# Two layers of graph attention on one core: the order in which layer 1's masks are loaded

## The chip, the core and the metric

One core of a Trainium2 chip runs the whole kernel in one launch. Its engines are TensorE (PE, with PEld for its weight loads), VectorE (DVE), ScalarE (ACT), GpSimd (POOL) and SyncE (SP), which here does nothing but issue DMAs; 16 DMA engines move the data. Each engine runs its own instructions in order and waits on semaphores for the others. The metric is the device time of one execution, in microseconds.

## The reference

`x` is 16 batches of 1024 nodes with 512 features, `adj` a 1024 x 1024 matrix with about one sixteenth of its entries set, all float32.

```python
# layer 0
h = relu(layernorm(x))
x = x + (adj @ h) @ weight + bias
# layer 1, with adj as the mask
u = relu(layernorm(x))
h = u @ W
e = leaky_relu((h @ a1)[:, :, None] + (h @ a2)[:, None, :], 0.2) * adj
att = softmax(e, axis=2)
x = x + elu(att @ h + beta * h)
```

The product of scores and mask is a plain multiplication, so each batch's 1024 x 1024 softmax needs the whole of `adj` (4 MB) again.

## The kernel before

The kernel handles layer 0 batch after batch, then layer 1 batch after batch. The change lies in layer 1. For each batch `b` there are two phases on TensorE. `layer1_a` multiplies the attention matrix by `u` (results named `z`), `layer1_b` multiplies the result by `W` (results named `pq`). Both use a scheme of seven products of half-size blocks instead of eight, in the order p1, p5, p2, p6, p7, p3, p4 for the weights and p1, p2, p6, p5, p7, p3, p4 for the attention. Each product has two parts, so a phase has 14 steps, numbered 0 to 13. The sums that the scheme needs of the right operand are T1 to T4 (tiles `pT_T`); T4 is built late, its first half after step 9 and its second after step 10 of `layer1_a` (`LATE_A`, line 1166), and product p4 reads it in steps 12 and 13.

While TensorE works on batch `b`, the other engines prepare the softmax of batch `b + 1`. Its work is cut into named pieces, which tables place behind numbered steps: `SOFTMAX_A` (line 1159) in `layer1_a`, `SOFTMAX_B` and `LOGITS_B` (lines 1164 and 1165) in `layer1_b`. A table's place fixes the order of the pieces on every engine. The pieces are:

- `L`: load the logits' two vectors. `L0` to `L7`: load one mask, 128 rows of 1024 numbers (512 KB), into the pool `ld`, which has two buffers of 4 KB per partition. `e0` to `e7`: the same load into the pool `b4`, which has 12 buffers of 4 KB, shared with the scores and the sums of `z` (lines 1150 and 1151).
- `M0` to `M7` (`masked`, line 753): ScalarE writes the scores `e` in four pieces, VectorE multiplies them by the mask and keeps the row maximum `mx`.
- `X` and `x` (`spread_max`): after M3 and after M7, the maxima of four blocks go to DRAM (`md`) and come back spread (`mall`), five DMAs. `N` and `n` (`top`) take the final maximum on VectorE (`nm`).
- `E0` to `E7`: exponentials on ScalarE, with row sums. `V0` to `V7`: transposes on VectorE into `pT`. `S` and `s` spread the sums (`sd`, `sall`), as `X` does.

SP gets all DMAs of these pieces in one order. With them stand, in `layer1_a`, the stores of the batch before (`out_dram<-o`, four DMAs after each of steps 3 to 6, line 923) and the loads of `u` (`ul_U`); in `layer1_b` of batches 1 to 8 a late row of batch 15 (`late`), which is loaded, normalised and stored again. POOL issues four DMAs per batch that add `x1d` to the output (`o<-x1d`, line 916), which run from the end of `layer1_b` into `layer1_a`. SP also waits, before most DMAs, for the DMA eight places earlier, since eight semaphores serve them in turn.

A load names its buffer's pool like this:

```python
def load(self, g, pl=None, tag="ld"):
    self.mask[g] = (pl or ld).tile([P, N], F32, tag=tag, name=f"mask_{self.b}_{g}")
    sp.dma_start(out=self.mask[g], in_=maskd[g])
```

The pool gives a new tile the buffer that came free, and the load waits until the last reader of that buffer is done. Nearly every instruction is recorded through one helper, so the profile shows line 118 throughout, and the tiles' names tell the instructions apart.

Of the kernel before, what the change touches and what calls it, by code (L numbers as in the profile page):

```python
# [65 lines left out]
def kernel(  # L66
# [12 lines left out]
    B, N, D = x.shape  # L79
# [996 lines left out]
    def merged(*plans):  # L1076
        out = {}
        for plan in plans:
            for k, steps in plan.items():
                out.setdefault(k, []).extend(steps)  # L1080
        return out
# [57 lines left out]
    def plan_softmax(order, s):  # L1139
        names = {  # L1140
            "L": [s.logits], "B": [s.blocks, 0], "b": [s.blocks, 1],
            "X": [s.spread_max, 0], "x": [s.spread_max, 1], "N": [s.top, 0], "n": [s.top, 1],
            "S": [s.spread_sum, 0], "s": [s.spread_sum, 1],
            "D": [s.diagonal, 0], "d": [s.diagonal, 1],
        }
        for g in range(NCH):
            names[f"M{g}"] = [s.masked, g]
            names[f"E{g}"] = [s.exp, g]
            names[f"V{g}"] = [s.turn, g]
            names[f"L{g}"] = [s.load, g]  # L1150
            names[f"e{g}"] = [s.load, g, b4, "b4"]
            names[f"K{g}"] = [s.keep, g]
            names[f"R{g}"] = [s.reload, g]
        for n in ("T1", "T2", "T3", "T4"):
            for k in range(2):
                names[n + "ab"[k]] = [s.right_sum, n, k]
        return {k: [tuple(names[n]) for n in steps.split()] for k, steps in order.items()}

    SOFTMAX_A = {
        0: "M0 L2 M1 L3", 1: "M2 L4", 2: "M3 L5 X", 3: "M4 L6", 4: "M5 L7", 5: "N B E0",  # L1160
        6: "M6 E1 V0", 7: "M7 x V1", 8: "E2", 9: "E3 V2 S", 10: "n b V3 E4", 11: "E5 V4",
        12: "E6 V5", 13: "E7 V6 V7 s",
    }
    SOFTMAX_B = {0: "D", 1: "T1a", 2: "T1b", 4: "d", 5: "T2a", 6: "T2b"}
    LOGITS_B = {8: "L", 11: "L0", 12: "L1"}
    LATE_A = {5: "T3a", 6: "T3b", 9: "T4a", 10: "T4b"}


# [21 lines left out]
    for b in range(B):  # L1190
# [14 lines left out]
        else:  # L1205
# [4 lines left out]
            plans_b += [  # L1210
                plan_softmax(FIRST_B, sms[0]), plan_softmax(LOGITS_B, sms[1]),
            ]
# [24 lines left out]
    for b in range(B):  # L1237
# [16 lines left out]
        if b + 2 < B:  # L1254
            plan_b = merged(plan_b, plan_softmax(LOGITS_B, sms[b + 2]))
        if 1 <= b <= NCH:
# [46 lines left out]
```

## Time and profile before

| | us |
|---|---|
| median of 3 runs | 2292.17 (2292.01 to 2292.51) |
| profiled execution | 2291.31 |
| its span, first to last instruction | 2289.5 |
| first `z` matmul of batch 0 | 1098.42 |
| last matmul | 2279.95 |

Times in the views count from the start of the span. Layer 1 is thus the second half, 16 batches. The granted TensorE clock was 0.998 of full speed. In the views, a line has the start, the duration, the engine, the operation, and the tiles as written and read; in square brackets stands how long the engine stood idle before it and what ended that wait. "SPq" lines are DMA issues, whose duration is that of issuing, not of the transfer. In the list of waits, a line gives the waiting engine and tile, what it waited for, the total in us, how often, and the longest. Idle time of an engine other than the bound costs nothing by itself.

### The profile page before, as it was taken

Reading aid. Unit: us, or ns where it says so; the run is one execution under the profiler, and the core shown is the slowest. Engines: PE = TensorE matmul, PEld = TensorE weight load, DVE = VectorE, ACT = ScalarE, POOL = GpSimd, SP = SyncE. Lnnn points to the kernel's source line nnn. Section 1 sums busy time; section 2 is a strip of 40 time slices with the busy share of each in tenths; the row PEclk is TensorE's granted clock in tenths of the full one; section 3 lists DMA queues with packets and bytes.
Section 4 is the critical chain, followed back from the end, with each engine's and each line's share of the span. In section 5 each row is a group of like instructions: output and inputs, shape, how many; then the busy total and the mean of one; then the engine's idle time right before and its main releaser. Section 6 shows DMA issues by size and latency. Waiting matters only on the chain.

```text
span 2289.5 us, 29757 instructions
## 1 busy us (share of the span) xinstructions
PE 2253.4 (98%) x8524; PEld 1609.9 (70%) x8524; DVE 1842.7 (80%) x4285; ACT 1540.5 (67%) x4106; POOL 244.0 (11%) x508
## 2 busy tenths in 40 slices
PE   9999999999999999999999999999999999999998
PEld 5888888888888888888566546664566556664565
DVE  7888888988888888889877777787678776787664
ACT  3776776777777767666577577766767677766653
POOL 1211111121111111110000000000000000000000
PEclk9999999999999999999999999999999999999999
DMA  7343454343344434336555566546655655446541
GB/s 215 130 139 120 139 169 157 129 148 127 123 148 157 163 133 149 98 109 210 168 138 143 152 172 165 145 144 170 177 142 144 178 154 147 133 133 167 160 122 54
DMA packets 194292, 336.03 MB, mean 147 GB/s; under 512 B 78800, under 2 KB 86992, under 8 KB 194128
## 3 DMA queue, kind: packets, MB, share of 16 engines
q1 hardware_dynamic: 185168, 302.15, 40.9%
q0 software_dynamic: 8640, 31.46, 7.4%
q8 instruction: 67, 1.10, 0.2%
q14 instruction: 97, 0.79, 0.1%
q10 hardware_dynamic: 320, 0.52, 0.1%
HBM read 228.33 MB, written 109.91 MB: 148 GB/s over the span
## 4 chain that ended last, share of the span: by engine, by line
PE 70%; DMA 12%; DVE 8%; ACT 5%; SPq 3%; issue 2%; POOL 1%; DVEq 0%; ACTq 0%; POOLq 0%
PE po_Y L118 9%; PE pq_Y L118 8%; PE y_Y L118 8%; PE z_Y L118 8%; DMA mask<-maskd 7%; PE po_X L118 5%; PE y_X L118 5%; PE pq_X L118 4%; DVE e L118 3%; DMA md<-mx 3%; SPq L118 3%; PE y_W L118 2%; PE pq_W L118 2%; PE y_p7y L118 2%; PE y_p3y L118 2%; PE po_W L118 2%
## 5 line engine op out<-in xcount | busy, mean ns | idle before, releaser
L118 ACT ACTIVATE e<-e,nm 128x256 f32<-128x256 f32 x480 | 237.1, 497 | 168.1 <-DVE nm L118 168.1
L118 DVE CUSTOM_DVE_ANT_0 e<-e,mask 128x256 f32<-128x256 f32 x512 | 190.8, 421 | 189.2 <-DMA mask<-maskd 161.8
L118 PE MATMUL z_Y<-pT,ul_U 128*128 128x512 f32 x512 | 224.9, 592 | 0.0
L118 ACT ACTIVATE e<-s2b,s1b 128x256 f32<-128x256 f32 x512 | 216.4, 500 | 0.0
L118 PE MATMUL po_Y<-w_c,y_C 128*128 128x256 f32 x768 | 188.3, 379 | 0.0
L118 PEld LDWEIGHTS z_Y<-pT,ul_U 128*128 128x128 f32 x512 | 97.1, 190 | 115.8 <-issue 112.0
L118 PE MATMUL pq_Y<-w_c,z_C 128*128 128x256 f32 x768 | 173.4, 379 | 0.0
L118 DVE CUSTOM_DVE_ANT_0 y_S<-xr,v_bc 128x512 f32<-128x512 f32 x240 | 165.2, 688 | 9.2 <-DVE s L118 0.5
L118 PEld LDWEIGHTS pq_Y<-w_c,z_C 128*128 128x128 f32 x768 | 145.9, 190 | 26.7 <-issue 7.7
L118 PEld LDWEIGHTS po_Y<-w_c,y_C 128*128 128x128 f32 x768 | 145.9, 190 | 20.3 <-ACT po_X L118 0.2
L118 DVE STREAM_TRANSPOSE pT<-e 128x512 f32<-128x512 f32 x240 | 155.5, 686 | 1.0
L118 PE MATMUL z_Y<-pT_T,ul_U 128*128 128x512 f32 x256 | 117.8, 605 | 20.1 <-DVE pT_T L118 20.1
L118 ACT ACTIVATE h<-h,nb_h,r_h 128x512 f32<-128x512 f32 (+1 forms) x132 | 98.2, 792 | 57.5 <-POOL nb_h L118 57.5
L118 POOL DMA_DIRECT2D o<-x1d x60 | 52.7, 936 | 620.7 <-DVE o L118 558.0
L118 ACT ACTIVATE y_S<-xr 128x512 f32<-128x512 f32 x90 | 56.7, 630 | 91.8 <-DVE xr L118 91.4
L118 PE MATMUL po_X<-w_c,y_S 128*128 128x256 f32 x512 | 115.7, 379 | 0.0
L118 PE MATMUL pq_X<-w_c,z_S 128*128 128x256 f32 x512 | 115.6, 379 | 0.0
L118 PE MATMUL z_X<-pT_T,ul_S 128*128 128x512 f32 x256 | 112.5, 592 | 0.0
L118 PE MATMUL z_W<-pT,ul_U 128*128 128x512 f32 x256 | 112.5, 592 | 0.0
L118 PE MATMUL z_Y<-pT_T,ul_S 128*128 128x512 f32 x256 | 112.5, 592 | 0.0
L118 PE MATMUL z_X<-pT,ul_S 128*128 128x512 f32 x256 | 112.5, 592 | 0.0
L118 PEld LDWEIGHTS z_Y<-pT_T,ul_U 128*128 128x128 f32 x256 | 48.0, 192 | 87.3 <-issue 52.7
(241 smaller groups left out, 5115.0 us busy)
## 6 DMA issues: line engine op xcount, KB each, us to landing
mask<-maskd SPq DMA_DIRECT2D x128, 512.0 KB
h<-in_x_dram SPq DMA_DIRECT2D x64, 512.0 KB
xr<-in_x_dram SPq DMA_DIRECT2D x256, 128.0 KB
x1d<-xr SPq DMA_DIRECT2D x64, 512.0 KB
ul_U<-ud_U SPq DMA_DIRECT2D x64, 512.0 KB
ud_U<-xr SPq DMA_DIRECT2D x60, 512.0 KB
o<-x1d POOLq DMA_DIRECT2D x60, 512.0 KB, 7.6
out_dram<-o SPq DMA_DIRECT2D x240, 128.0 KB
```

The source lines that it names most:

```text
L118: return lambda *args, **kwargs: tc.keep_in_program_order(f(*args, **kwargs))
```

## The change

Only two tables differ. The loads of masks 2 and 3 move into the weight product of the batch before, into `b4`; there `L0` and `L1` move two steps forward. Masks 4 and 5, still in `ld`, take the places of 2 and 3 behind M0 and M1. Masks 6 and 7 go into `b4` behind steps 1 and 2, ahead of the row maximum `X` and of the output's stores, which begin behind step 3. The tables are also used once at the end of layer 0, for batch 1's masks.

```diff
     SOFTMAX_A = {
-        0: "M0 L2 M1 L3", 1: "M2 L4", 2: "M3 L5 X", 3: "M4 L6", 4: "M5 L7", 5: "N B E0",
+        0: "M0 L4 M1 L5", 1: "M2 e6", 2: "M3 e7 X", 3: "M4", 4: "M5", 5: "N B E0",
         6: "M6 E1 V0", 7: "M7 x V1", 8: "E2", 9: "E3 V2 S", 10: "n b V3 E4", 11: "E5 V4",
         12: "E6 V5", 13: "E7 V6 V7 s",
     }
     SOFTMAX_B = {0: "D", 1: "T1a", 2: "T1b", 4: "d", 5: "T2a", 6: "T2b"}
-    LOGITS_B = {8: "L", 11: "L0", 12: "L1"}
+    LOGITS_B = {8: "L", 9: "L0", 10: "L1", 11: "e2", 12: "e3"}
     LATE_A = {5: "T3a", 6: "T3b", 9: "T4a", 10: "T4b"}
```

## The prediction

> **What bounds the kernel now.** I read the page's busy times first, then the waits, then the timelines of TensorE, VectorE and the DMA queue over one batch of layer 1, and last the busy table by stretches for the DMA engines.
>
> ```profile
> PE 2253.4 (98%) x8524; PEld 1609.9 (70%) x8524; DVE 1842.7 (80%) x4285; ACT 1540.5 (67%) x4106; POOL 244.0 (11%) x508
> ```
>
> ```profile
> DVE e L118 <- DMA mask<-maskd: 161.8, 50, 6.1
> ...
> PE z_Y L118 <- DVE pT_T L118: 20.1, 14, 3.0
> ```
>
> TensorE is the bound, so only its own gaps are worth anything: the 161.8 us that VectorE stands before missing masks count only where they make TensorE late. The last line says where: the matmuls of the right sum T4 (tile `pT_T`), 14 times. The page's 20.1 us is the gap alone; the loss is better taken from the distance between the first `z` matmuls of successive batches. Batches 0 and 1 take 72.24 us each (seven products of 6.87 and seven of 3.45 us) and have no gap. Batches 2 to 14 take 78.25, 74.38, 73.90, 73.28, 75.25, 75.02, 73.86, 73.41, 73.10, 73.47, 73.23, 74.28, 73.21: together 25.5 us over 72.24 each. That is all this change can take away; batch 15 prepares no softmax.
>
> I follow batch 3, whose first `z` matmul starts at 1321.15 ("rel 0"). TensorE first:
>
> ```profile
> 1362.35 1.88 PE L118 MATMUL z_Y<-pT_T,ul_U 128*128 128x512 f32 x4
> 1366.10 5.42 PE L118 MATMUL z_Y<-pT_T,ul_U 128*128 128x512 f32 x12 [1.87 <-DVE pT_T L118]
> ```
>
> Product p4 starts at rel 41.2 and uses the first half of T4 for 4 matmuls; the second half is due at 41.2 + 1.7 = rel 42.9, and comes at 44.9. VectorE shows why:
>
> ```profile
> 1335.55 0.42 DVE L118 CUSTOM_DVE_ANT_0 e<-e,mask 128x256 f32<-128x256 f32 x1 [5.04 <-DMA mask<-maskd]
> ...
> 1347.37 0.26 DVE L118 TENSOR_REDUCE nm<-mall 128x16 f32<-128x64 f32 x1 [0.51 <-DMA mall<-md]
> ...
> 1353.38 0.42 DVE L118 CUSTOM_DVE_ANT_0 e<-e,mask 128x256 f32<-128x256 f32 x1 [4.41 <-DMA mask<-maskd]
> ...
> 1359.87 1.20 DVE L118 TENSOR_TENSOR pT_T<-pT,pT_T 128x1024 f32<-128x1024 f32 x1
> ...
> 1364.83 1.22 DVE L118 TENSOR_TENSOR pT_T<-pT,pT_T 128x1024 f32<-128x1024 f32 x1
> ```
>
> M6 (1353.38) waits 4.41 us for its mask; behind it without a further wait stand V0, M7, V1, the reads of p7, T4's first half, V2, the reads of p3 and T4's second half. The queue shows why the mask is late:
>
> ```profile
> 1309.45 0.90 SPq L118 DMA_DIRECT2D mask<-maskd  x2
> ...
> 1328.35 11.85 SPq L118 DMA_DIRECT2D mask<-maskd  x4
> 1340.24 0.42 SPq L118 DMA_DIRECT2D md<-mx  x1
> 1344.32 1.74 SPq L118 DMA_DIRECT2D mall<-md  x4
> 1346.16 1.78 SPq L118 DMA_DIRECT2D out_dram<-o  x4
> 1348.05 0.38 SPq L118 DMA_DIRECT2D mask<-maskd  x1
> ```
>
> Masks 0 and 1 go early; 2 to 5 each wait for M0 to M3 to free one of the two `ld` buffers; 6 goes behind `mall` and an output store, though its buffer was free since M4. The DMA engines are idle just before and full in that stretch (the last two columns are DMA share and GB/s):
>
> ```profile
> 1314.00:1319.00 5.00, 5.00 (x25) 4.38 (x25) 4.27 (x8) 3.98 (x10) 1.82 (x4) 1.00 0.00 0
> 1325.00:1340.00 15.00, 15.00 (x36) 6.65 (x35) 7.53 (x36) 12.42 (x31) 2.60 (x3) 1.00 1.03 241
> ```
>
> **What the Trainium skill says.** "DMA: Bandwidth & Descriptors", section Queues, rings and completion order: a DMA engine consumes one ring's descriptors in ring order and takes turns between rows packet by packet. The trace agrees: mask packets and POOL's accumulating ones alternate from 1332 to 1334 (0.17 and 0.33 us each), and `md`, 8 KB, takes 4.1 us from issue to `mall` behind mask 5, where `sd`, equally small, took 1.4 us at 1299.76 on a quiet queue. "PSUM — Partial Sum Buffer", section Engine vs sequencer instructions, calls VectorE's queue strict FIFO; T4 behind M6 is that. "Perfetto Trace Analysis", section Optimization Strategy: the same gap repeating on the engine that should be saturated can mean too few buffers for the next tile; 13 batches with one gap at one place agree.
>
> **The change part by part.** No instruction and no byte is added. In the program's order, VectorE's, TensorE's and POOL's instructions stand as before; only SP's order, the 4 KB slots, and so some waits of SP and ScalarE, differ.
>
> (a) Masks 2 and 3 move up behind masks 0 and 1, at about 1310.4 and 1310.9, from 1328.35 and 1329.94. They pass the late row's store and then M0 and M1. Two masks took from 1310.5 to 1313.5, so these run to about 1316.5, in the idle stretch, and are there 10 us before M2. Their slots were last held by score tiles whose transposes end at about 1301: no wait. The late store (1319.11) finds the queue empty again. M2 and M3 then wait only for ScalarE, which writes their scores from 1329.85 and 1332.13: M3 ends at about 1332.13 + 0.45 + 1.6 = 1334.2 (rel 13.1) instead of rel 18.6.
>
> (b) Masks 4 and 5 take the places of 2 and 3 behind M0 and M1 (rel 7.2 and 8.8), so as those did they land at rel 14.4 and 17.2. ScalarE writes M4's and M5's scores at rel 14.4 and 17.9: cost nothing.
>
> (c) Masks 6 and 7 follow at once, at about rel 9.2 and 9.7, in slots whose TensorE readers ended in the weight product: no wait. They leave the stores' stretch (share 0.9 and more from 1350 to 1360). M6 waits only for ScalarE.
>
> (d) The row maximum `md`, issued at rel 13.2 instead of 19.1, now stands behind four masks. This is the unknown cost. From 1331.5 the engines have to move the rest of POOL's third accumulation and the fourth (2.6 us each, 128 packets of 0.33 us on 16 engines) and four masks (1.3 us each): 10.4 us, to about rel 20.8; with some 1 us for `md` itself it lands near rel 21.8. Before, its landing is `mall`'s issue, rel 23.2. At the low end `md` comes at rel 19, at the high end one mask later than before, 24.5; I take 1.3 us earlier than before. `mall` and the maxima follow at their old distance, so the first exponential, at rel 26.7 before, starts at 25.4.
>
> (e) From there ScalarE sets the pace. In batch 0, where masks weren't late, M6 starts 3.0 us after the first exponential (E0), M7 7.0 and T4 ends 17.1 us after it (E0 25.2, T4 42.3). So E0 by rel 42.9 - 17.1 = 25.8 leaves no gap. The old starts of E0 in batches 2 to 14 are 27.9, 26.7, 26.2, 25.8, 27.6, 27.6, 25.9, 25.8, 25.4, 26.2, 24.8, 26.3, 25.6. With (d)'s 1.3 us off, only batches 2, 6 and 7 are left over, by 0.8 + 0.5 + 0.5 = 1.8 us. With nothing off, 2.1 + 0.9 + 0.4 + 1.8 + 1.8 + 0.1 + 0.4 + 0.5 = 8.0 us remain.
>
> (f) New waits on ScalarE: M7's scores now go into mask 6's slot and wait for M6. In ScalarE's order E1 (2.0 us) and a copy (0.5) lie between M6's scores and M7's, M6's last piece on VectorE ends 0.4 us after its scores: hidden with 2 us to spare. If mask 6 were late, ScalarE would stop there, with E2, E3 and the copies of `z` behind it. The copy of p6 waits for the late store, landed some 12 us before: nothing.
>
> (g) Batch 0: masks 2 and 3 also pass the four `x1d` stores and the load of W1, due much later. The queue is full from rel -1.4 to 14.1 in both orders; masks 4 to 7 end near 19.3, `md` near 20.4 (before, `mall` at 21.3): no gap appears.
>
> Sum: 25.5 - 1.8 = 23.7, less 0.7 for spread between batches: 23.0 us. The profiled execution, 2291.31 us (span 2289.5), becomes 2268.3; the median of the runs is 0.86 above it, so 2269.2.
>
> **Rivals.** B, `md` gains nothing behind four masks: 8.0 us of gaps stay, 17.5 gained, 2274.7. For it: `md` in ring order; against: masks 2 and 3 run in an idle stretch. C, the gap refills: VectorE, freed, meets another late operand, or mask slots bind, and half or more stays: 2281 to 2292. Against it: slots resolve a step or more before their users, and batch 1, already without a gap, has T4 at 42.5. That the change doesn't bring masks earlier belongs here. D, slower: `md` much later behind four masks and the accumulations. The old T4 ends are on average 42.9 + 25.5/13 = rel 44.9, which E0 reaches at 27.8; old E0 is 26.3 on average, so it decides where `md` lands over 1.5 us later than before, at about rel 24 on average. At 2.5 us later, 13 batches lose 1.0 us each: 2305. For it: 2 MB now stand before `md`; against: nothing was added to those stretches and 1 MB left them.
>
> **How the numbers follow.** Likeliest, 0.62: 2266.7 (all 25.5 gone) to 2272, at 2269.2. B 0.20, 2272 to 2280. C 0.11, of which 0.05 still gains over 0.2% and 0.06 doesn't. D 0.07. 0.2%, 4.6 us, is about what a measurement of this kernel can tell from no change. Faster 0.62 + 0.20 + 0.05 = 0.87, same 0.06, slower 0.07. Range: 2266 to 2280 holds the first two.
>
> **What would show it.** Right: masks 2 and 3 issued with 0 and 1; no wait of M2, M3 and M6 for a mask; `mall` about 1.3 us earlier; batches of 72.2 to 73 us. Wrong: `mall` at rel 23 or later (B, D), or gaps of TensorE at another tile (C).

## The result and the profile after

| | before, us | after, us |
|---|---|---|
| median (range), 4 runs each | 2292.09 (2288.11 to 2292.51) | 2266.95 (2266.72 to 2267.59) |
| profiled execution | 2291.31 | 2266.74 |
| its span | 2289.5 | 2264.4 |
| batches 0 to 14, time beyond 72.24 us each, summed | 25.5 | under 0.1 |
| E0, mean of batches 2 to 14, rel | 26.30 | 24.51 |
| T4 ends, mean of the same, rel | 44.59 | 42.11 |

The changed kernel takes 0.9895 [0.9877, 0.9912] of the time before. The medians differ by 25.1 us, where 22.9 were forecast; all that layer 1 lost is gone. ("rel" is, as in the prediction, the time after a batch's first `z` matmul; E0 is the first exponential; T4's second half is due at rel 42.75, as a run below shows.)

The busy times of the page of the changed kernel, for the row shown of before:

```profile
PE 2248.3 (99%) x8524; PEld 1611.9 (71%) x8524; DVE 1858.7 (82%) x4285; ACT 1540.4 (68%) x4106; POOL 244.0 (11%) x508
```

The same instructions take about the same busy time; the span around them is shorter. Where it went is told by the shares of the chain that ended last, first of before, then of after:

```profile
PE 70%; DMA 12%; DVE 8%; ACT 5%; SPq 3%; issue 2%; POOL 1%; DVEq 0%; ACTq 0%; POOLq 0%
```

```profile
PE 96%; DVE 2%; ACT 1%; DMA 1%; issue 0%; POOL 0%; SPq 0%; DVEq 0%; ACTq 0%; POOLq 0%
```

Before, the chain left TensorE again and again for a mask or a row maximum and the engines behind it. After, it is TensorE almost from end to end. That a chain has 12% of DMA does not mean that 12% can be had: the share counts all the time since the chain turned to the DMA, and most of it lay beside matmuls that ran anyway. The gain was 1.1%.

The waits of the changed kernel:

```profile
DVE e L118 <- ACT e L118: 97.0, 85, 1.9
...
DVE nm L118 <- DMA mall<-md: 38.9, 15, 3.8
...
DVE e L118 <- DMA mask<-maskd: 3.2, 3, 1.4
...
PEld z_Y L118 <- DVE pT_T L118: 1.6, 4, 0.6
```

VectorE's 161.8 us before masks are 3.2. Little of that time turned into work (VectorE is busy for 1858.7 us, before 1842.7): it now waits 97.0 us for ScalarE's scores, which costs nothing. The gaps of TensorE before T4 are not in the list any more; its weight loads still wait four times, 1.6 us in all, which says how near the edge the changed kernel stands.

Batch 3 of the changed kernel begins at 1315.56. TensorE's timeline, at p1, p4 and the first `z` matmul of batch 4:

```profile
1315.56 7.03 PE L118 MATMUL z_Y<-pT,ul_U 128*128 128x512 f32 x16
...
1356.76 7.03 PE L118 MATMUL z_Y<-pT_T,ul_U 128*128 128x512 f32 x16
...
1387.80 7.03 PE L118 MATMUL z_Y<-pT,ul_U 128*128 128x512 f32 x16
```

p4 starts at rel 41.2 as before, but its 16 matmuls are one group instead of 4 and 12 with 1.87 us between, and the batch takes 72.24 us. The DMA queue of the same stretch shows the order that the change makes:

```profile
1304.59 1.85 SPq L118 DMA_DIRECT2D mask<-maskd  x4
...
1322.75 3.14 SPq L118 DMA_DIRECT2D mask<-maskd  x4
1328.74 0.32 SPq L118 DMA_DIRECT2D md<-mx  x1
1337.36 1.74 SPq L118 DMA_DIRECT2D mall<-md  x4
1339.22 6.29 SPq L118 DMA_DIRECT2D out_dram<-o  x12
```

Four masks from rel -11.0, the other four from rel 7.2 (instead of 11.85 us of issues that waited for buffers), the row maximum at rel 13.2, its answer at rel 21.8, then twelve stores with no mask among them. The two steps by which the table moves masks 0 and 1 forward show nothing: mask 0 was issued at rel -11.7 before. The busy table by stretches (the last two columns are DMA share and GB/s):

```profile
1306.00:1309.00 3.00, 3.00 (x16) 2.64 (x15) 0.77 (x2) 1.05 (x3) 0.00 (x0) 1.00 0.95 369
1309.00:1314.00 5.00, 5.00 (x25) 4.41 (x24) 4.78 (x9) 3.99 (x9) 1.81 (x4) 1.00 0.46 185
1320.00:1335.00 15.00, 15.00 (x37) 6.64 (x36) 12.07 (x51) 12.41 (x30) 2.33 (x3) 1.00 1.02 255
```

The stretch that had a share of 0.00 is now about half used. The one from about rel 4 is as full as it was (1.02, before 1.03), with masks that are issued earlier. VectorE, last:

```profile
1340.47 0.26 DVE L118 TENSOR_REDUCE nm<-mall 128x16 f32<-128x64 f32 x1 [3.75 <-DMA mall<-md]
...
1343.96 0.42 DVE L118 CUSTOM_DVE_ANT_0 e<-e,mask 128x256 f32<-128x256 f32 x1 [1.90 <-ACT e L118]
...
1356.91 1.22 DVE L118 TENSOR_TENSOR pT_T<-pT,pT_T 128x1024 f32<-128x1024 f32 x1
```

VectorE now stands 3.75 us before the row maximum (before, 0.51), so that DMA is the latest thing there. M6, the middle line, waits for its scores, no more for its mask. T4 ends at 1358.13, rel 42.6.

### The profile page after: what moved, and what is told of

Same layout as the page of the kernel before. It is cut to its first block, busy times and chain, and to the rows that moved or that the text cites. A ratio compares the mean times of both kernels' runs of the same rounds, so it can differ in the third digit from the quotient of the medians.

```text
span 2264.4 us, 29788 instructions
## 1 busy us (share of the span) xinstructions
PE 2248.3 (99%) x8524; PEld 1611.9 (71%) x8524; DVE 1858.7 (82%) x4285; ACT 1540.4 (68%) x4106; POOL 244.0 (11%) x508
## 3 DMA queue, kind: packets, MB, share of 16 engines
q1 hardware_dynamic: 185168, 302.15, 41.2%
## 4 chain that ended last, share of the span: by engine, by line
PE 96%; DVE 2%; ACT 1%; DMA 1%; issue 0%; POOL 0%; SPq 0%; DVEq 0%; ACTq 0%; POOLq 0%
PE z_Y L118 19%; PE z_X L118 10%; PE pq_Y L118 9%; PE po_Y L118 9%; PE y_Y L118 8%; PE z_W L118 5%; PE pq_X L118 5%; PE po_X L118 5%; PE y_X L118 4%; PE y_W L118 2%; PE pq_W L118 2%; PE po_W L118 2%; PE y_p3y L118 2%; PE y_p7y L118 2%; PE y_p4y L118 2%; PE y_p6y L118 2%
## 5 line engine op out<-in xcount | busy, mean ns | idle before, releaser
L118 DVE CUSTOM_DVE_ANT_0 e<-e,mask 128x256 f32<-128x256 f32 x512 | 203.2, 425 | 100.2 <-ACT e L118 97.0
L118 PE MATMUL z_Y<-pT_T,ul_U 128*128 128x512 f32 x256 | 112.5, 592 | 0.0
L118 PEld LDWEIGHTS po_X<-w_c,y_S 128*128 128x128 f32 x512 | 97.4, 190 | 13.1
```

Of the source, the lines that this page charges most:

```text
L118: return lambda *args, **kwargs: tc.keep_in_program_order(f(*args, **kwargs))
```

## The experiments

The question was which of the two moves brings the gain, and whether the order of the row maximum among the masks matters. Under "gaps" stands the time of batches 0 to 14 beyond 72.24 us each, summed, in the profiled execution; E0 and T4 are means of batches 2 to 14 (rel); ratios are to the kernel before on the same chip. The medians are of 4 executions, of 12 for e4 and 20 for e6.

| run | median, us | ratio [95%] | gaps | E0 | T4 ends, mean / latest |
|---|---|---|---|---|---|
| e1_early_only | 2265.86 | 0.9878 [0.9863, 0.9893] | 0 | 22.37 | 41.88 / 42.31 |
| e2_ahead_only | 2308.18 | 1.0062 [1.0047, 1.0077] | 43.0 | 28.38 | 45.54 / 49.48 |
| e3_ahead_max_first | 2276.87 | 0.9923 [0.9907, 0.9940] | 11.1 | 26.36 | 43.52 / 45.52 |
| e4_pool_only | 2293.88 | 0.9991 [0.9980, 1.0002] | 27.5 | 26.30 | 44.66 / 46.71 |
| e5_max_first | 2266.40 | 0.9866 [0.9842, 0.9890] | 0 | 22.25 | 41.85 / 41.85 |
| e6_ballast2 | 2291.05 | 0.9980 [0.9971, 0.9990] | 22.5 | 27.09 | 44.25 / 45.30 |
| e7_ballast4 | 2332.69 | 1.0154 [1.0124, 1.0184] | 69.0 | 29.61 | 46.77 / 48.25 |
| e8_ballast2_max_first | 2266.67 | 0.9873 [0.9854, 0.9893] | 0.9 | 24.70 | 42.26 / 43.20 |
| e9_ballast2_behind | 2267.20 | 0.9876 [0.9859, 0.9892] | 0.7 | 24.64 | 42.20 / 43.42 |
| e10_changed_again | 2266.69 | 0.9874 [0.9858, 0.9890] | 0.9 | 24.60 | 42.14 / 43.37 |

The medians of before were 2295.39 beside e1 to e4, 2295.52 beside e5 to e7 and 2294.75 beside e8 to e10. Beside e10 the change gained 28.1 us, not 25.1: the medians of the kernel before differ more between the measurements (2292.09 to 2295.52) than those of the changed one (2266.95 and 2266.69).

### Masks 2 to 5 early, 6 and 7 left where they were

Against the changed kernel:

```diff
-        0: "M0 L4 M1 L5", 1: "M2 e6", 2: "M3 e7 X", 3: "M4", 4: "M5", 5: "N B E0",
+        0: "M0 L4 M1 L5", 1: "M2", 2: "M3 X", 3: "M4 L6", 4: "M5 L7", 5: "N B E0",
```

> Masks 2 and 3 early and 4 and 5 in their old places, but masks 6 and 7 back in the pool ld, behind the row maximum and the first two output stores. Theory (T4 follows the start of the exponentials E0, which follows md in the one DMA ring): md now stands behind two masks and not four, mall is issued near rel 18, E0 near rel 21.5; mask 6 is issued near rel 20 to 21 and lands near 25, so M7 starts before rel 31 and T4 ends by rel 42: no gap is left, about 2267 us. Rival (the stores in front of masks 6 and 7 are the cause): M6 still waits behind the stores until about rel 31 and most gaps stay, 2280 to 2290 us.

Measured 2265.86 us, no gap. The queue of batch 3 of this run (first `z` matmul at 1315.48):

```profile
1328.66 0.32 SPq L118 DMA_DIRECT2D md<-mx  x1
1334.74 1.74 SPq L118 DMA_DIRECT2D mall<-md  x4
1336.60 1.96 SPq L118 DMA_DIRECT2D out_dram<-o  x4
1338.66 0.37 SPq L118 DMA_DIRECT2D mask<-maskd  x1
```

Mask 6 still stands behind `mall` and a store, and VectorE still waits 47.5 us in all for masks. But `mall` is issued at rel 19.3 instead of 23.2, and the mask behind it at rel 23.2 instead of 26.9. So the second half of the change, masks 6 and 7 in front of the stores, isn't needed for the gain: bringing the row maximum forward pulls the late masks along, since they stand in the same queue. The rival, that the stores in front of mask 6 cost the time, falls as the cause by itself.

### Masks 6 and 7 ahead, as in the change, but 2 and 3 not early

Against the kernel before:

```diff
-        0: "M0 L2 M1 L3", 1: "M2 L4", 2: "M3 L5 X", 3: "M4 L6", 4: "M5 L7", 5: "N B E0",
+        0: "M0 L2 M1 L3", 1: "M2 L4 e6", 2: "M3 L5 e7 X", 3: "M4", 4: "M5", 5: "N B E0",
```

> Only masks 6 and 7 moved ahead of the row maximum and the stores, as in the change; masks 0 to 5 as before. Theory: M6 has its mask, but md, issued at rel 19 as before, now stands behind mask 7 and part of mask 6 too, so E0 comes about 1.3 us later than before; with T4's end at E0 + 17.1 and due at 42.9 the gaps come to about 24 us: about 2291 us, no gain. Rival (the stores in front of masks 6 and 7 are the cause): most of the gaps go, 2267 to 2275 us.

Slower than before, by 0.6%, where about no change was expected. E0 came 2.1 us later than before, not 1.3: on average over batches 2 to 14 `md` waited 4.9 us for its answer, before 3.3, and was issued 0.4 us later. And a gap opened that the expectation didn't have, in batch 2 for instance. TensorE, with p7 in the first two lines and p4 in the last, and VectorE at the same place:

```profile
1276.26 1.96 PE L118 MATMUL z_Y<-pT,ul_U 128*128 128x512 f32 x4 [2.48 <-DVE pT L118]
1279.62 5.42 PE L118 MATMUL z_Y<-pT,ul_U 128*128 128x512 f32 x12 [1.40 <-DVE pT L118]
...
1295.68 7.11 PE L118 MATMUL z_Y<-pT_T,ul_U 128*128 128x512 f32 x12 [2.06 <-DVE pT_T L118]
```

```profile
1273.50 0.43 DVE L118 CUSTOM_DVE_ANT_0 e<-e,mask 128x256 f32<-128x256 f32 x1 [2.88 <-DMA mask<-maskd]
...
1274.89 1.22 DVE L118 TENSOR_TENSOR pT<-pT,pT 128x1024 f32<-128x1024 f32 x1
1277.97 0.26 DVE L118 TENSOR_REDUCE nm<-mall 128x16 f32<-128x64 f32 x1 [1.85 <-DMA mall<-md]
...
1278.35 1.22 DVE L118 TENSOR_TENSOR pT<-pT,pT 128x1024 f32<-128x1024 f32 x1
```

The sum T3 (it is written in the place of tile `pT`) has one half before the maximum `nm` and one behind it in VectorE's order. The first half was late because M5, ahead of it, waited 2.88 us for its mask; the second because the maximum waited 1.85 us for `mall`. So a late row maximum makes a second gap, at p7, besides the one at p4. It comes out of the gap at p4 and is not added to it: the ends of T4 beyond rel 42.75 (the next run) sum to 39.7 us, and two stretches at half clock, 1.7 us each (last section), make it 43.1, against 43.0 measured.

### The same with the row maximum ahead of masks 6 and 7

Against the kernel before:

```diff
-        0: "M0 L2 M1 L3", 1: "M2 L4", 2: "M3 L5 X", 3: "M4 L6", 4: "M5 L7", 5: "N B E0",
+        0: "M0 L2 M1 L3", 1: "M2 L4", 2: "M3 L5 X e6 e7", 3: "M4", 4: "M5", 5: "N B E0",
```

> As the run with masks 6 and 7 alone ahead of the stores, but the row maximum's DMAs are issued before these two masks. Theory: md and E0 come as before the change (E0 at rel 26.2 on average), M6 and M7 have their masks; the gaps that stay are the excess of E0 over rel 25.8, 8.0 us in sum: about 2275 us. This is the number of the case in which the maximum gains nothing. Rival (ring order of md does not matter): the same time as with the masks ahead of the maximum.

2276.87 us, 31.3 less than the run above, for another place in the queue of two masks (in the run above, mask 6 also stood ahead of mask 5). E0 stays where it was before (26.36, before 26.30), while VectorE's waits for masks fall by 60 us. Some waits of this run:

```profile
DVE e L118 <- DMA mask<-maskd: 101.6, 31, 6.8
...
PE z_Y L118 <- DVE pT_T L118: 8.1, 8, 2.1
```

The gaps fall from 25.5 to 11.1 us. This splits the loss of the kernel before: 14.4 us need only masks 6 and 7 in time, the other 11.1 need an earlier row maximum. (1.7 of the 14.4 are matmuls at half clock, last section.) It also gives the moment at which T4's second half is due. With rel 42.9, as the prediction had it, T4's ends in this run give 9.8 us of gaps; with 42.75 they give the measured 11.1.

### Masks 6 and 7 in the other pool, at the old place in the queue

Against the kernel before:

```diff
-        0: "M0 L2 M1 L3", 1: "M2 L4", 2: "M3 L5 X", 3: "M4 L6", 4: "M5 L7", 5: "N B E0",
+        0: "M0 L2 M1 L3", 1: "M2 L4", 2: "M3 L5 X", 3: "M4 e6", 4: "M5 e7", 5: "N B E0",
```

> Masks 6 and 7 get buffers of the 4 KB pool, but every load stands in its old place in SP's order. Theory: their old buffers in ld had been free since M4 and M5, so nothing changes: 2292 us. Rival (two buffers were too few for masks 6 and 7): they come earlier, and gaps go, 2270 to 2285 us.

Nothing changed within what can be measured, 0.9991 [0.9980, 1.0002], and the waits stayed: 152.7 us for masks, before 161.8. More buffers bring nothing to these two loads, whose place in the queue is late. A gap that repeats at one place, which the prediction read as agreeing with too few buffers, does not tell the two causes apart. For masks 2 and 3 it is not shown that buffers bring nothing: before, they waited for one of the two buffers of `ld`, and they could go early only because `b4` had room. No run gave them the room and kept their place.

### The changed kernel with the row maximum ahead of masks 6 and 7

Against the changed kernel:

```diff
-        0: "M0 L4 M1 L5", 1: "M2 e6", 2: "M3 e7 X", 3: "M4", 4: "M5", 5: "N B E0",
+        0: "M0 L4 M1 L5", 1: "M2", 2: "M3 X e6 e7", 3: "M4", 4: "M5", 5: "N B E0",
```

> The changed kernel with the row maximum's DMAs issued ahead of masks 6 and 7. Theory: md stands behind masks 4 and 5 alone, so mall is issued near rel 19 (21 in the changed kernel) and E0 near rel 22.5; but no gap is left to remove, so the time is that of the changed kernel, 2266 to 2268 us. Rival (the engines' pace, not the maximum, holds T4): the same time, but T4 ends no earlier either where it ended after rel 42.

The same time, since no gap was left to take. But E0 comes 2.3 us earlier than in the changed kernel, and T4 ends at rel 41.85 in every batch. VectorE of batch 3 (from 1316.09) shows what holds it there:

```profile
1354.05 0.69 DVE L118 TENSOR_TENSOR z_C<-z_X,z_C 128x512 f32<-128x512 f32 x1 [0.40 <-PE z_X L118]
...
1356.71 1.22 DVE L118 TENSOR_TENSOR pT_T<-pT,pT_T 128x1024 f32<-128x1024 f32 x1
```

VectorE now waits for TensorE's product p3, whose reads stand ahead of T4's second half. The softmax is no longer what sets T4. The margin to the due moment is 0.9 us in all batches, where the changed kernel had none in its worst (42.77 in batch 7).

### Two and four copies of 512 KB ahead of the row maximum

Against the changed kernel; the second run has `range(4)`. The copies go from `maskd` to a scratch tensor in DRAM and serve only as load:

```diff
+        def ballast(self):
+            for k in range(2):
+                sp.dma_start(out=ed[k], in_=maskd[k])
...
+        names["Z"] = [s.ballast]
...
-        0: "M0 L4 M1 L5", 1: "M2 e6", 2: "M3 e7 X", 3: "M4", 4: "M5", 5: "N B E0",
+        0: "M0 L4 M1 L5", 1: "M2 e6", 2: "M3 e7 Z X", 3: "M4", 4: "M5", 5: "N B E0",
```

> The changed kernel with two extra copies of 512 KB from DRAM to DRAM in the queue just ahead of the row maximum; they move data that nobody reads. Theory: each holds md back by at least a mask's 1.3 us, together 2.6 us; with the changed kernel's starts of E0 and T4 at E0 + 17.1 due at 42.9, the gaps come to 18 us: about 2285 us, and the sum of gaps follows the measured starts of E0 whatever the copies cost. Rival (md has slack, the gaps came from the late masks alone): 2267 us.

> The same with four extra copies. Theory: 5.2 us later, every batch from 0 to 14 has a gap, 57 us in sum: about 2324 us; with the maximum later than rel 27.5 a second gap appears earlier in the batch, at product p7, whose sum T3 stands behind the maximum on VectorE, and it takes part of the gap at T4. Rival: 2267 us.

E0 moved by 2.6 and 5.1 us, 1.3 for each copy, as expected (with four copies 1.0 of the 5.1 is that `md` itself was issued later, at rel 14.2 on average); T4 followed it at a distance of 17.16 to 17.17 us on average in e2, e3, e6 and e7. The times came out above what was expected, 2291.05 for 2285 and 2332.69 for 2324. The queue in batch 3 of the run with two copies (its first `z` matmul at 1320.45):

```profile
1327.64 3.14 SPq L118 DMA_DIRECT2D mask<-maskd  x4
1330.83 1.32 SPq L118 DMA_DIRECT2D ed<-maskd  x2
1333.63 0.33 SPq L118 DMA_DIRECT2D md<-mx  x1
1344.81 1.74 SPq L118 DMA_DIRECT2D mall<-md  x4
```

All the masks are issued as in the changed kernel and `md` again at rel 13.2, but its answer comes at rel 24.4. That alone returns the kernel to within 0.2% of before. With four copies both gaps are there; waits of that run:

```profile
DVE nm L118 <- DMA mall<-md: 116.3, 15, 8.9
...
PE z_Y L118 <- DVE pT_T L118: 29.2, 15, 2.1
PE z_Y L118 <- DVE pT L118: 19.8, 14, 2.9
```

The maximum is waited for 116.3 us in all, and TensorE waits at p4 and, in nearly every batch, at p7. Two terms that the expectations lacked come near the excess: the due moment, 0.15 us earlier in 15 batches (2.2 us), and matmuls at half clock after a gap, 1.7 us each time (last section), once in the run with two copies and seven times in the one with four. Together 3.9 and 14.1 us; the profiled executions, 2288.17 and 2336.70, were 3.2 and 12.7 above what was expected.

### The same two copies with the row maximum ahead of masks 6 and 7, and behind the row maximum

A rival was that the copies' traffic, not their place, delays everything. Against the run with two copies:

```diff
-        0: "M0 L4 M1 L5", 1: "M2 e6", 2: "M3 e7 Z X", 3: "M4", 4: "M5", 5: "N B E0",
+        0: "M0 L4 M1 L5", 1: "M2", 2: "M3 Z X e6 e7", 3: "M4", 4: "M5", 5: "N B E0",
```

```diff
-        0: "M0 L4 M1 L5", 1: "M2 e6", 2: "M3 e7 Z X", 3: "M4", 4: "M5", 5: "N B E0",
+        0: "M0 L4 M1 L5", 1: "M2 e6", 2: "M3 e7 X Z", 3: "M4", 4: "M5", 5: "N B E0",
```

> The two extra copies of 512 KB stand ahead of the row maximum, but masks 6 and 7 behind it: the same DMAs as in the run with two copies, in another order. Theory: md waits for as much data as in the changed kernel (two masks and two copies in place of four masks, with the copies dearer), E0 near rel 25 on average, so few gaps or none: 2267 to 2272 us, against 2291 with masks 6 and 7 ahead as well. Rival (the load of the extra copies on the DMA engines and not the place of md makes the gaps): about 2290 us again.

> The two extra copies stand just behind the row maximum's DMAs instead of ahead of them, ahead of the output's stores. Theory: md and E0 come as in the changed kernel, the stores and the second half's md come up to 3 us later, which has time: 2266 to 2268 us. Rival (load and not place): about 2290 us.

> The changed kernel itself beside the two controls, for a comparison on one chip: about 2267 us by every theory.

Both runs move the same bytes in `layer1_a` as the run at 2291.05, and take 2266.67 and 2267.20; the changed kernel beside them 2266.69. The queue of the first (batch 3 from 1315.70), then of the second (from 1314.67):

```profile
1324.85 1.12 SPq L118 DMA_DIRECT2D ed<-maskd  x2
1328.88 0.32 SPq L118 DMA_DIRECT2D md<-mx  x1
1337.56 1.91 SPq L118 DMA_DIRECT2D mall<-md  x4
1339.58 0.84 SPq L118 DMA_DIRECT2D mask<-maskd  x2
```

```profile
1327.85 0.32 SPq L118 DMA_DIRECT2D md<-mx  x1
1336.76 1.92 SPq L118 DMA_DIRECT2D mall<-md  x4
1338.73 1.11 SPq L118 DMA_DIRECT2D ed<-maskd  x2
```

In both, `md` has four transfers of 512 KB ahead of it as in the changed kernel, and is answered after 8.7 and 8.9 us, as there (8.6). Two copies behind it cost nothing. So what counts is how many bytes stand ahead of `md` in its own queue, not how many the batch moves. From its issue to its answer `md` takes, on average over batches 2 to 14, 5.4 us with two masks ahead (masks 2 to 5 early), 7.7 with four (the changed kernel) and 10.2 with four masks and two copies, about 1.2 us for each 512 KB. The Trainium skill, "DMA: Bandwidth & Descriptors", section Queues, rings and completion order, says that each DMA engine consumes the descriptors of one ring in ring order; the runs agree and add this price. POOL's accumulations, on another queue, ran in the same stretch in all these runs; no run varied them.

The repeat of the changed kernel also shows its spread: in this execution E0 is at rel 26.2 and 25.9 in two batches, T4 ends at up to 43.37, and 0.9 us of gaps is back. No version was measurably faster than the changed kernel. With the row maximum ahead of masks 6 and 7, or with these two left at their old place, the time is the same and the margin larger.

## Why the prediction was right

**What bounds.** Right: 25.5 us lost before one half of T4 was named as all that the change could take, and it took all of it. The medians moved by 25.1. Not all of it was gap: 1.7 us in batch 2 were matmuls at half clock (last section).

**(a), (b), masks 2 to 5.** Right. They are issued in the idle stretch and at rel 7.2; M2 and M3 stop waiting for masks, and the row maximum `md` is issued at rel 13.2, as worked out. The run with these two moves alone shows that they are enough.

**(c), masks 6 and 7.** They leave the stores' stretch and M6 waits only for ScalarE, as predicted. That this part carries any of the gain, which the prediction left unsaid, the runs deny: without it the time is the same, and without (a) and (b) it costs 0.6%. Behind an unmoved row maximum the same two loads did bring 14.4 of the 25.5 us, but what they bring there is contained in what (a) and (b) bring.

**(d), the row maximum behind four masks.** The mechanism was right. In batch 3 `mall` came at rel 21.8 and E0 at 25.4, the two numbers of the prediction, and not by chance: from rel 10.35 until the answer the packets took 10.2 us of the 16 engines (4.6 of them POOL's, nearly all the rest SP's), where 10.4 had been summed. What failed is that one batch stood for all. `md` was issued between rel 17.5 and 21.3 in batches 2 to 14 before, and is issued at 13.2 in every one now, so the batches that were latest gain most: E0 came 1.8 us earlier on average, not 1.3, and 2.0 to 2.5 us in batches 2, 6 and 7.

**(e), the pace of ScalarE.** The 17.1 us from E0 to T4's end held in every run in which E0 set it (17.16). Two small terms were off. T4 is due at rel 42.75, not 42.9, so the limit for E0 is 25.6. And the 1.8 us left over with the 0.7 for spread were mis-sized: together under 0.1 us in layer 1, because the three batches left over are those in which (d) gained most. (The profiled execution gained 24.6 us of the 25.5: layer 1 starts 0.4 us later, and 0.5 us more lie outside the span.) That so little is left is partly luck: the latest E0, at rel 25.61 in batch 7, lies on the limit. In the repeated execution two batches were beyond it and 0.9 us was back, so a residue of this kind exists, but smaller than was set down.

**(f), (g).** Right: where E0 sets T4, T4 keeps its distance from it (17.16 us in batch 3), so nothing is added on ScalarE, and batch 0 takes 72.24 us.

**The rivals.** B's mechanism is shown by the kernel with masks 6 and 7 behind an unmoved row maximum: 11.1 us of gaps for the 8.0 predicted, 2276.87 us for 2274.7. D's is real as well: with two copies ahead, E0 averaged rel 27.09 and 22.5 us of gaps were back; at 28.38, with masks 6 and 7 ahead but 2 and 3 not early, the kernel was slower than before. D did not have the second gap, at p7, which takes part of the one at p4. The changed kernel escaped D because masks 2 and 3 had left the queue in front of `md`, so that M3 ends and `md` is issued 6.2 us earlier on average, of which its longer way takes back 4.4. C's other late operand exists, VectorE's wait for p3, but it holds T4 only at rel 41.85, 0.9 us before T4 is due, so no gap came of it.

## What to carry to other kernels

Where one queue carries both bulk loads and a small transfer on which a whole chain waits, order it by who is waited for: count the bytes ahead of the small one, move bulk that is needed later behind it, and bulk that can go early into an idle stretch. A load that is late may be late by its place in the queue and not for want of a buffer; ask what stands ahead of it before giving it more memory. Memory is worth giving where it lets a load move to an idle stretch, as masks 2 and 3 did. When the bounding engine has no gap left, two versions of equal time differ in margin, and how far the last input stands from its due moment tells which to keep.

## What the runs showed of the hardware

Some gaps of TensorE cost more than their length. Batch 2 of the kernel before lost 6.01 us. Its timeline of TensorE at p4:

```profile
1285.05 1.98 PE L118 MATMUL z_Y<-pT_T,ul_U 128*128 128x512 f32 x4 [0.79 <-DVE pT_T L118]
1290.03 7.11 PE L118 MATMUL z_Y<-pT_T,ul_U 128*128 128x512 f32 x12 [2.99 <-DVE pT_T L118]
```

The twelve matmuls behind the second gap take 7.11 us, where those of batch 3 took 5.42: 1.69 us of the loss are not gap but slow matmuls. The busy table by stretches tells why (third column from the end: the granted clock):

```profile
1284.10:1290.00 5.90, 2.15 (x5) 0.68 (x4) 5.83 (x9) 0.00 (x0) 0.00 (x0) 1.00 0.37 97
1290.40:1293.70 3.30, 3.30 (x5) 1.33 (x4) 3.23 (x6) 3.30 (x13) 0.00 (x0) 0.50 0.40 101
```

TensorE was busy for 2.15 of 5.90 us, and the clock then stood at 0.50; the record is 3.413 us long. The Trainium skill, "TensorE: Matmul & The Clock Gate", section Part 1: The HAM clock gate (the "warmup" mystery), gives half rate after an idle window of about 3.4 us, and a free-running window of 3413 ns. The length agrees, and in the run with four copies the slow records start whole multiples of 3.413 us apart (78.51 us is 23 of them). But the idle times that sufficed were shorter than a window, and their length alone doesn't decide. From the timeline of that run, two of its p4:

```profile
1531.09 5.42 PE L118 MATMUL z_Y<-pT_T,ul_U 128*128 128x512 f32 x12 [2.06 <-DVE pT_T L118]
...
1607.30 7.11 PE L118 MATMUL z_Y<-pT_T,ul_U 128*128 128x512 f32 x12 [2.06 <-DVE pT_T L118]
```

The same 2.06 us are free of the penalty once and cost 1.69 us more the other time. Where the gap falls tells them apart. Each trace's own clock records fix a grid of windows of 3.413 us. On it, the first gap is split, 0.79 us into one window and 1.27 into the next; the second lies whole in one. The busy table for these three windows (TensorE's busy time is the first number behind the comma):

```profile
1526.40:1529.82 3.42, 2.63 (x7) 0.84 (x5) 3.35 (x7) 0.00 (x0) 0.00 (x0) 1.00 0.53 160
1529.82:1533.23 3.41, 2.14 (x5) 1.06 (x6) 3.34 (x8) 1.78 (x7) 0.00 (x0) 1.00 0.12 8
1604.91:1608.32 3.41, 1.35 (x4) 0.55 (x4) 3.38 (x7) 0.66 (x3) 0.00 (x0) 1.00 0.24 64
```

Half clock follows the last of them, at 1608.32. The same holds in all twelve traces: between 30 and 2250 us, away from the start and the end of the program, there are twelve half-clock records, each 3.413 us long, and each follows a window in which TensorE was idle for 2.06 us or more (2.99 in the kernel before, 2.95 in the run with masks 6 and 7 in the other pool). No window with less idle time is followed by one; the longest of these, in the run with four copies, has 2.00 us. The sums are those of the profile, which models the ends of matmuls, and no run was made to place a gap. So a gap of about 2 us or more on a saturated TensorE is best counted with a risk of 1.7 us on top; shorter ones cost only their length here.
